# Query projections of head pairs by seven products, and values made per group, in a decoder layer on one core

## The chip, the cores and the metric

The kernel runs on one core of one Trainium2 chip. The metric is the device time of one execution in microseconds. Before the change three runs gave 1305.65, 1307.67 and 1308.76 us; their median, 1307.67, is the time before. The core's engines are called as the profile calls them: PE (TensorE matmul), PEld (its weight load), DVE (VectorE), ACT (ScalarE), POOL (GpSimd) and SP (SyncE, which issues most DMAs).

## What is computed

The reference is one decoder layer on 1024 positions of width 512, all in float32: attention with 32 query heads and 8 key and value heads of width 128, rotary positions and a causal mask; a layer norm; a gated feed-forward part of inner width 1792; a second layer norm.

```
q = (x @ wq)  -> 32 heads;   k = (x @ wk), v = (x @ wv) -> 8 heads
q = q * cos + rotate_half(q) * sin;   k likewise
att = softmax(mask(q k^T / sqrt(128)));   out = (att v) @ wo
x = layernorm(x + out)
n = rmsnorm(x) * ln_w
x = layernorm(x + down(silu(gate n) * up n))
```

Each key and value head serves four query heads, which are called a group here; there are eight groups, 0 to 7.

## The kernel before

Positions are cut into eight tiles of 128 (`T`, `NT`) and each tile into four blocks of 32 rows (`Q`). One step of the attention, a slot, takes 32 positions of all four heads of a group as one 128-row product: `scores(g, t, ...)` multiplies `qT[:, t]` (four heads x 32 positions) with the keys up to that position, DVE adds the mask and takes the row minimum (`low`), ACT takes the exponential, DVE the reciprocal of its sum, ACT scales, DVE transposes in 32x32 blocks (`turned`). After four slots a tile is whole; 16 DMAs on SP bring it into position order (`gather`, `moved`), and PE multiplies it with the values (`o`). Two tiles then go together through the output projection, as seven products for a two by two block product (`project_pair`), added into `sums` by DVE. Tiles are taken in the order 7, 1, 5, 3, 4, 2, 6, 0 in every group.

PE's instructions stand in the order in which the program emits them. The other engines' order is set by a scheduler, close to the program's order. A small planner decides what PE does between the scores of one slot and the next. It counts in units of about one 512-wide matmul call. Work is of two kinds. `Late` pieces are the value product and output projection of a tile whose gather should have landed. `Early` pieces are the projections for the next group, as a fixed list from `projections(g + 1)` and the values. Each slot has a budget, its share by weight of all units of the group; the weight of block t is 1 - share + 2 share (t + 1) / 33, with share 0.25 for groups 0 to 5. In `run`, late work that is due comes first, then early work up to a pace (`early.total * passed / slots`, `passed` being the weights so far). Early work behind `must` (the total less 2.5 units for each slot still to come) is emitted at the slot's end whether there is room or not, so after a group's last slot all of it is out. Groups 6 and 7 use `deal`, which spreads what is left.

`project` makes one projection of 512 positions of one head: four calls over the four 128-row chunks of x (`xT`), then on DVE the product with the cosines (L335) and, halves swapped, with the sines (L337, L338), all read from PSUM, then on POOL the sum of both (L339). A group's list is: both halves of the keys, the queries of four heads for positions 512 to 1023, then for 0 to 511. Queries of a group fill one of two buffers `qTs` (pool `qp`). `values` (L298) makes the values of two groups at once: x's 128 positions are the weights, and 256 columns of `wv` move. It is called in portions of four or eight tiles.

Before the first group, `xT` and the first weights are loaded on the queues of SP and ACT, and PE projects the keys and queries of group 0 in full: 40 calls. PSUM has four single banks for projections, outputs and values (`mbank`) and two double banks for scores (`pair`): scores of one slot reuse the bank of the slot two before, when ACT has taken its exponential. The queue of SP also carries the weights, issued when the tile that they go to is to be free. The feed-forward part follows after the eight groups and runs PE with products of 512 columns to the end.

## Time and profile before

| what | value |
|---|---|
| runs | 1305.65, 1307.67, 1308.76 us (median 1307.67) |
| profiled execution | 1307.23 us, span 1305.4 us |
| PE busy | 1288.0 us, 99% of the span |
| DVE, ACT, POOL busy | 754.3, 463.0, 346.6 us |
| mean granted PE clock | 0.995 |
| start up to the first scores | 40.45 us |
| a group in the middle (2 to 5) | 125 to 126 us |
| longest waits of PE (s for ACT p) | 8.9 us in 6 waits, all in groups 6 and 7 |

Busy PE is a pipelined measure: a 512-wide instruction is recorded as 0.59 us long but follows the one before by 0.43 us. So the time of a stream of matmuls is read from starts. A call in the program is two instructions in these rows, as the operands are float32. Idle time of DVE, ACT and POOL costs nothing by itself; what counts is whether PE, whose order is fixed, finds its operands and its bank ready.

### The profile page before, as it was taken

Reading aid. Unit: us, or ns where it says so; the run is one execution under the profiler, and the core shown is the slowest. Engines: PE = TensorE matmul, PEld = TensorE weight load, DVE = VectorE, ACT = ScalarE, POOL = GpSimd, SP = SyncE. Lnnn points to the kernel's source line nnn. Section 1 sums busy time; section 2 is a strip of 40 time slices with the busy share of each in tenths; the row PEclk is TensorE's granted clock in tenths of the full one; section 3 lists DMA queues with packets and bytes.
Section 4 is the critical chain, followed back from the end, with each engine's and each line's share of the span. In section 5 each row is a group of like instructions: output and inputs, shape, how many; then the busy total and the mean of one; then the engine's idle time right before and its main releaser. Section 6 shows DMA issues by size and latency. Waiting matters only on the chain. (4 is left out here: it accounts for less than half of the span.)

```text
span 1305.4 us, 13447 instructions
## 1 busy us (share of the span) xinstructions
PE 1288.0 (99%) x3842; PEld 717.6 (55%) x3842; DVE 754.3 (58%) x1570; ACT 463.0 (35%) x927; POOL 346.6 (27%) x557
## 2 busy tenths in 40 slices
PE   9999999999999999999999999999999999999998
PEld 4655655655565556555655565554656544444445
DVE  4666566566656775577567656666656564244122
ACT  0443344434443444344444443445454021121000
POOL 6222214112312331242123212331411444423000
PEclk9999999999999999999999999999999999999999
DMA  8242324334333433343234323444344511100000
GB/s 281 69 113 69 89 77 125 81 98 114 96 85 90 113 92 82 89 126 93 73 88 114 91 71 81 122 105 108 92 106 112 179 37 49 44 17 1 16 25 24
DMA packets 102120, 115.48 MB, mean 88 GB/s; under 512 B 18976, under 2 KB 77088, under 8 KB 102048
## 3 DMA queue, kind: packets, MB, share of 16 engines
q1 hardware_dynamic: 101040, 112.67, 32.8%
q10 hardware_dynamic: 1008, 1.97, 0.4%
q8 instruction: 31, 0.51, 0.2%
q14 instruction: 41, 0.34, 0.1%
HBM read 37.23 MB, written 2.10 MB: 30 GB/s over the span
## 5 line engine op out<-in xcount | busy, mean ns | idle before, releaser
L401 ACT ACTIVATE p<-s,low 128x928 f32<-128x928 f32 (+31 forms) x256 | 179.2, 700 | 457.0 <-DVE low L387 425.1
L132 PE MATMUL s<-kT,qT 128*128 128x512 f32 (+15 forms) x768 | 271.8, 464 | 8.9 <-ACT p L401 8.9
L132 PE MATMUL o<-moved,v 128*128 128x512 f32 x550 | 258.5, 599 | 0.0
L409 DVE STREAM_TRANSPOSE turned<-p 128x1024 f32<-128x1024 f32 (+7 forms) x244 | 186.7, 775 | 100.8 <-ACT p L406 84.5
L132 PE MATMUL q_ps<-xT,wq 128*128 128x512 f32 x512 | 240.2, 594 | 0.0
L132 PEld LDWEIGHTS s<-kT,qT 128*128 128x128 f32 x768 | 145.4, 190 | 159.6 <-issue 131.5
L387 DVE CUSTOM_DVE_ANT_0 s<-s,mask 128x928 f32<-128x928 f32 (+31 forms) x256 | 179.7, 704 | 64.0 <-PE s L132 62.2
L406 ACT ACTIVATE p<-p,share 128x928 f32<-128x928 f32 (+31 forms) x256 | 186.0, 734 | 56.5 <-DVE share L405 56.4
L132 PEld LDWEIGHTS o<-moved,v 128*128 128x128 f32 x550 | 103.2, 191 | 103.9 <-issue 97.9
L339 POOL TENSOR_TENSOR qT<-qT,q_b 128x512 f32<-128x512 f32 x64 | 81.0, 1267 | 239.4 <-DVE q_b L338 237.4
L132 PEld LDWEIGHTS q_ps<-xT,wq 128*128 128x128 f32 x512 | 95.6, 191 | 86.8 <-issue 80.8
L405 DVE RECIPROCAL share<-total 128x1 f32<-128x1 f32 x256 | 40.9, 160 | 146.2 <-ACT p L401 145.1
L132 PE MATMUL y<-wo,oT 128*128 128x256 f32 x428 | 104.5, 380 | 0.0
L399 POOL MEMSET p<- 128x96 f32 (+2 forms) x192 | 26.9, 152 | 271.0 <-DVE turned L409 232.3
L132 PE MATMUL f<-wd,hT 128*128 128x512 f32 (+1 forms) x252 | 96.4, 545 | 0.0
L132 PEld LDWEIGHTS y<-wo,oT 128*128 128x128 f32 x428 | 80.0, 190 | 19.9 <-issue 7.3
L132 PEld LDWEIGHTS f<-wd,hT 128*128 128x128 f32 x252 | 47.9, 190 | 48.8 <-issue 47.1
L555 DVE TENSOR_TENSOR sums<-y,sums 128x512 f32<-128x512 f32 x112 | 68.4, 613 | 9.3 <-PE y L132 6.4
L132 PE MATMUL v_ps<-wv,xT 128*128 128x256 f32 x256 | 62.1, 379 | 0.0
L335 DVE TENSOR_TENSOR qT<-q_ps,cos 128x512 f32<-128x512 f32 x64 | 44.0, 687 | 30.0 <-PE q_ps L132 19.2
L132 PE MATMUL k_ps<-xT,wk 128*128 128x512 f32 x128 | 60.2, 593 | 0.0
L132 PEld LDWEIGHTS v_ps<-wv,xT 128*128 128x128 f32 x256 | 48.6, 190 | 16.1 <-issue 8.5
(143 smaller groups left out, 1198.8 us busy)
## 6 DMA issues: line engine op xcount, KB each, us to landing
moved<-turned SPq DMA_DIRECT2D x112, 128.0 KB, 2.4
moved<-turned SPq DMA_DIRECT2D x128, 112.0 KB, 2.2
moved<-turned SPq DMA_DIRECT2D x112, 96.0 KB, 2.1
moved<-turned SPq DMA_DIRECT2D x112, 80.0 KB, 2.1
wq<-wq SPq DMA_DIRECT2D x32, 256.0 KB, 2.8
wo<-wo SPq DMA_DIRECT2D x32, 256.0 KB, 2.9
moved<-turned SPq DMA_DIRECT2D x128, 64.0 KB, 2.0
moved<-turned SPq DMA_DIRECT2D x128, 48.0 KB, 1.9
```

What stands on the lines that cost most here:

```text
L132: tc.keep_in_program_order(nc.tensor.matmul(*args, **kw))
L335: nc.vector.tensor_tensor(dst, like(ps), like(cos[:, ts]), ALU.mult)
L339: nc.gpsimd.tensor_tensor(dst, dst, like(b), ALU.add)
L387: nc.vector.tensor_tensor_reduce(out=s[:, :n], in0=s[:, :n], in1=mask[:, T - n :], scale=1.0, scalar=MASKED, op0=ALU.add, op1=ALU.min, acc ...
L399: nc.gpsimd.memset(p[:, n:full], 0.0)
L401: nc.scalar.activation(p[:, :n], s[:, :n], AF.Exp, bias=low, scale=-1.0, accum_out=total)
L405: nc.vector.reciprocal(share, total)
L406: last_of_all = nc.scalar.activation(p[:, :n], p[:, :n], AF.Copy, scale=share)
L409: nc.vector.transpose(x[:, :, :, b, :].rearrange("p b j q -> p j b q"), p[:, :full].rearrange("p (j b k) -> p j b k", b=B, k=Q),)
L555: pin(nc.vector.tensor_tensor(to, out, to, ALU.add))
```

## The change

For two heads and all positions a query projection is a two by two block product: positions in two halves, x's 512 features in two halves, two heads. The change computes it with seven products and sums (Strassen's scheme in Winograd's form) where eight products stood: `project_two` issues seven products of two calls each. Fifteen of the sixteen head pairs go this way; the last two heads of group 7 stay with `project`.

The two halves of the positions are now the odd and the even tiles (x, cosines and sines are reordered so). The blocks a11, a12 (odd) and a22 (even) and the sums s1 to s4 of x are formed by DVE once at the start and kept; a21 itself isn't kept. Where the plain product of the even tiles is wanted, `operands` gives s1 and a22, and the weight's second half is replaced by its difference to the first, on POOL (`difference`). The sums of the weights of a pair (u1 to u4) are formed on POOL by `weigh`, for the next pair, after product p4. The order of products is p1, p2, p6, p5, p7, p4, p3. From them come c11 (odd, first head), c22 (even, second), c21 (even, first) and c12 (odd, second), in that order. Each is added up by DVE, in place of a read of PSUM by the rotation, and then rotated where it stands (`rotate`); c12 comes after p3, the last.

Queries are kept in three buffers of half a group each, taken in turn by `queries`: the even tiles' queries of the next group take the place of the odd ones of this group. So the planner holds early work back (`odd`) until the four odd tiles have had their scores. Values are made for one group at a time, in two pieces (odd and even tiles) with 128 columns moving, and copied by ACT once a piece. A group's early list is: keys odd, values odd, keys even, values even, then two head pairs; 44 units, where it was 48. Before the first group PE makes keys and queries of group 0 in 36 calls.

Loads of `wq`, `wk` and `wv` are issued at the end of the last use of what they replace. In the last group one spare tile in the place of x holds what had been in two tiles. Tiles in the feed-forward part change places; its products stay.

```diff
-OWN = [0] * (KV - 1) + [2]
+OWN = 2
+BY = 3
...
-    qp = pool("qp", 2)
+    qp = pool("qp", 1)
...
-    cp = pool("cp", 11)
+    cp = pool("cp", 9)
...
-        xT = wide.tile([P, NC, T], F32, tag="wide", name="xT")
+        blocks = wide.tile([P, 7, NC // 2, W], F32, tag="wide", name="blocks")
+        a11, a12, a22, s1, s2, s3, s4 = (blocks[:, n] for n in range(7))
+        a21 = s3
...
+        def weigh(n):
+            if 2 * n >= HEADS - OWN:
+                return
+            a, b = wqs[2 * n], wqs[2 * n + 1]
+            b11, b21, b12, b22 = a[:, :2], a[:, 2:], b[:, :2], b[:, 2:]
+            t = ap.tile([P, 3, NC // 2, HD], F32, tag="uq", bufs=1, name=f"uq{n}")
+            u1, u2, u4, u3 = t[:, 0], t[:, 1], t[:, 2], b12
+            nc.gpsimd.tensor_tensor(u1, b12, b11, ALU.subtract)
+            nc.gpsimd.tensor_tensor(u3, b22, b12, ALU.subtract)
+            nc.gpsimd.tensor_tensor(u2, b22, u1, ALU.subtract)
+            nc.gpsimd.tensor_tensor(u4, b21, u2, ALU.subtract)
+            sums_of[n] = b11, b21, b22, u1, u2, u3, u4
+
+        def difference(w):
+            nc.gpsimd.tensor_tensor(w[:, 2:], w[:, 2:], w[:, :2], ALU.subtract)
+
+        def operands(w, even):
+            x1, x2 = (s1, a22) if even else (a11, a12)
+            return [(w[:, c], (x1 if c < 2 else x2)[:, c % 2]) for c in range(NC)]
...
+        def load_block(queue_of, block, half, c):
+            queue_of.dma_start(
+                block[:, c % 2], x_t[c * P : (c + 1) * P, half * W : (half + 1) * W]
+            )
 
         load_wq(0)
-        load_xT(nc.scalar, 1, 0)
-        load_xT(nc.sync, 1, 1)
-        load_xT(nc.scalar, 1, 2)
+        load_block(nc.scalar, a11, 0, 0)
+        load_block(nc.sync, a11, 0, 1)
+        load_block(nc.scalar, a12, 0, 2)
         load_wk(0)
-        load_xT(nc.scalar, 1, 3)
+        load_block(nc.scalar, a12, 0, 3)
+        for c in range(NC):
+            load_block((nc.scalar, nc.sync)[c % 2], a21 if c < 2 else a22, 1, c)
+        load_wq(1)
         nc.sync.dma_start(sin, rope_sin)
         nc.scalar.dma_start(cos, rope_cos)
-        for c in range(NC):
-            load_xT(nc.scalar if c % 2 == 0 else nc.sync, 0, c)
-        for n in range(1, REP):
-            load_wq(n)
+        load_wq(2)
+        load_wq(3)
         load_wv(0)
-        load_wk(1)
         load_wo(0)
...
+        kTs, vs = {}, {}
+        held_q = qp.tile([P, 3, T // 2 // Q, REP, Q], F32, tag="q", name="queries")
+        def queries(g, even):
+            return held_q[:, (2 * g + even) % 3]
+        nc.vector.tensor_tensor(s1, a21, a22, ALU.add)
+        nc.vector.tensor_tensor(s3, a11, a21, ALU.subtract)
+        nc.vector.tensor_tensor(s2, s1, a11, ALU.subtract)
+        nc.vector.tensor_tensor(s4, a12, s2, ALU.subtract)
+        weigh(0)
+        def values(g, even):
+            if g not in vs:
+                vs[g] = piece(f"v{g}").rearrange("p (j f) -> p j f", j=NT)
+            if even:
+                difference(wvs[g])
+            pv = mbank(f"v_ps{g}_{even}")
+            for j in range(NT // 2):
+                for c, (w, x) in enumerate(operands(wvs[g], even)):
+                    matmul(
+                        pv[:, j * HD : (j + 1) * HD],
+                        lhsT=x[:, j * P : (j + 1) * P],
+                        rhs=w,
+                        start=(c == 0),
+                        stop=(c == NC - 1),
+                    )
+                if j == NT // 2 - 1:
+                    nc.scalar.copy(
+                        vs[g][:, 1 - even :: 2, :], pv.rearrange("p (j f) -> p j f", f=HD)
+                    )
+                    if even:
+                        load_wv(g + 1)
+                yield NC * HD / W
...
+        def rotate(dst, src, even, name):
+            ts = slice(even * W, (even + 1) * W)
+            b = ap.tile([P, W], F32, tag="rope_b", name=f"{name}_b{even}")
+            def swapped():
+                for to, of in ((slice(0, 64), slice(64, P)), (slice(64, P), slice(0, 64))):
+                    nc.vector.tensor_tensor(
+                        alike(b, dst)[to], src[of], alike(sin[:, ts], dst)[of], ALU.mult
+                    )
+            if src is dst:
+                swapped()
+            nc.vector.tensor_tensor(dst, src, alike(cos[:, ts], dst), ALU.mult)
+            if src is not dst:
+                swapped()
+            nc.gpsimd.tensor_tensor(dst, dst, alike(b, dst), ALU.add)
...
+        def project(dst, w, even, name):
+
+            if even:
+                difference(w)
+            ps = mbank(f"{name}_ps{even}")
+            for c, (w_c, x_c) in enumerate(operands(w, even)):
+                matmul(ps, lhsT=w_c, rhs=x_c, start=(c == 0), stop=(c == NC - 1))
                 if c < NC - 1:
                     yield 1
-            b = ap.tile([P, W], F32, tag="rope_b", name=f"{name}_b{h}")
-            shape = "p (n q) -> p n q"
...
+            dst = kTs[g].rearrange("p (n q) -> p n q", q=P)[:, 1 - even :: 2, :]
+            yield from project(dst, wks[g], even, f"k{g}")
+            if even:
+                load_wk(g + 1)
+        def project_queries(g, head, even):
+            dst = queries(g, even)[:, :, head, :]
+            yield from project(dst, wqs[g * REP + head], even, f"q{g}_{head}")
+        def project_two(g, n):
+            b11, b21, b22, u1, u2, u3, u4 = sums_of[g * 2 + n]
+            u = f"{g}_{n}"
+            v = ap.tile([P, W], F32, tag="v", bufs=1, name=f"qv{u}")
+            c11, c12, c21, c22 = (
+                queries(g, even)[:, :, 2 * n + h, :] for even in range(2) for h in range(2)
+            )
+            v_q = alike(v, c11)
+            ps = {}
+            products = (
+                (1, b11, a11), (2, b21, a12), (6, u2, s2), (5, u1, s1), (7, u3, s3),
+                (4, u4, a22), (3, b22, s4),
+            )
+            for k, w, x in products:
+                ps[k] = mbank(f"q{u}_p{k}")
+                q = alike(ps[k], c11)
+                for c in range(NC // 2):
+                    matmul(
+                        ps[k], lhsT=w[:, c], rhs=x[:, c], start=c == 0, stop=c == NC // 2 - 1
+                    )
+                    if c < NC // 2 - 1:
+                        yield 1
+                if k == 1:
+                    nc.scalar.copy(v, ps[1])
+                elif k == 2:
+                    nc.vector.tensor_tensor(c11, q, v_q, ALU.add)
+                    rotate(c11, c11, 0, f"q{u}_0")
+                elif k == 6:
+                    nc.vector.tensor_tensor(v, ps[6], v, ALU.add)
+                elif k == 5:
+                    nc.vector.tensor_tensor(c12, q, v_q, ALU.add)
+                elif k == 7:
+                    nc.vector.tensor_tensor(v, ps[7], v, ALU.add)
+                    nc.vector.tensor_tensor(c22, alike(ps[5], c22), v_q, ALU.add)
+                    rotate(c22, c22, 1, f"q{u}_1")
+                elif k == 4:
+                    nc.vector.tensor_tensor(c21, q, v_q, ALU.add)
+                    rotate(c21, c21, 1, f"q{u}_0")
+                    weigh(g * 2 + n + 1)
+                else:
+                    nc.vector.tensor_tensor(c12, q, c12, ALU.add)
+                    rotate(c12, c12, 0, f"q{u}_1")
+                    for h in range(2):
+                        load_wq((g + 1) * REP + 2 * n + h)
+                yield 1
...
+            pieces = [(NC, f(g, even)) for even in range(2) for f in (project_keys, values)]
+            pieces[1::2] = [(NT // 2 * NC * HD / W, p) for _, p in pieces[1::2]]
+            for n in range(REP // 2):
+                if 2 * (g * 2 + n) < HEADS - OWN:
+                    pieces.append((PAIR * 2, project_two(g, n)))
+                else:
+                    pieces += [(NC, project_queries(g, 2 * n + h, 0)) for h in range(2)]
+            return pieces
...
                 k1 = min(n, k0 + W)
                 matmul(
                     s[:, k0:k1],
-                    lhsT=qT[:, t, :, :].rearrange("p h q -> p (h q)"),
+                    lhsT=queries(g, i % 2 == 0)[:, i // 2 * B + b].rearrange("p h q -> p (h q)"),
...
+                if first and keep and k == 2:
+                    both[g, k] = [rows(f"held{k}_{n}") for n in range(2)]
                 elif first:
+                    if keep:
+                        t = piece(f"held{k}")
+                    else:
+                        t = ap.tile([P, 2 * W], F32, tag="oT", name=f"oT{u}")
+                    both[g, k] = [t[:, :W], t[:, W:]]
+                oT = both[g, k][p % 2]
...
+        def deal(early, limit, coming, weights, must, cap):
...
+                elif early.done < min(cap, early.there()):
...
-        keys, queries = projections(0)[:2], projections(0)[2:]
-        for _, piece_of in queries[:1] + keys[::-1] + queries[1:]:
-            for _ in piece_of:
+        pieces = [piece_of for _, piece_of in projections(0)]
+        for _ in range(4):
+            next(pieces[4])
+        for k in (0, 2, 4, 5):
+            for _ in pieces[k]:
                 pass
         for g in range(KV):
-            todo = [(NC, project_queries(g, a, 0)) for a in range(REP - OWN[g], REP)]
-            own = NC * OWN[g]
+            todo, own, odd = [], 0, math.inf
             if g == 0:
-                todo += some_values(0, range(NT))
+                todo += [(NT // 2 * NC * HD / W, values(0, even)) for even in range(2)]
...
             if g + 1 < KV:
+                odd = sum(units for units, _ in todo) + 2 * (NC + NT // 2 * NC * HD / W) + 9
                 todo += projections(g + 1)
-            m = g // 2 + 1
-            if m < KV // 2:
-                half = some_values(m, range(4) if g % 2 == 0 else range(4, NT))
-                todo[-3:-3] = half
+            else:
+                todo += [(NC, project_queries(g, a, 1)) for a in range(REP - OWN, REP)]
+                own = NC * OWN
             early = Early(todo, held if g == KV - 1 else ())
...
-                if p == 1 and g % 2 == 0 and g // 2 + 1 < KV // 2:
-                    load_wv(g // 2 + 1)
-                if p == 4 and g + 2 < KV:
-                    load_wk(g + 2)
...
-                        run(due, early, pace, must, LEAST)
+                        if g == 0:
+                            must = max(must, min(NC * 2, done))
+                        run(due, early, pace, must, LEAST, odd if done < slots // 2 else None)
-                        deal(early, limit, coming, weights[done - 1 :], own * min(1, done / 3))
+                        must = own * min(1, done / BY)
+                        cap = min(limit, odd) if done < slots // 2 else limit
+                        deal(early, limit, coming, weights[done - 1 :], must, cap)
...
-        nT = wide.tile([P, NC, T], F32, tag="wide", name="nT")
+        normed = wide.tile([P, 7, T], F32, tag="wide", name="normed")
+        nT = normed[:, :NC]
...
+
+    order = np.arange(T).reshape(NT // 2, 2, P)[:, ::-1].transpose(1, 0, 2).ravel()
+        "x_t": given["L0_attn_x"].reshape(T, HID)[order].T,
+        "rope_cos": cos[:, order],
+        "rope_sin": sin[:, order],
```

## The prediction, made before the changed kernel had run

> **What bounds the kernel now.** I read the page first: busy time by engine, then the costliest groups. TensorE (PE) is busy for 1288.0 of 1305.4 us. In the group rows, DVE and POOL sit beside it with idle time of their own.
>
> ```profile
> PE 1288.0 (99%) x3842; PEld 717.6 (55%) x3842; DVE 754.3 (58%) x1570; ACT 463.0 (35%) x927; POOL 346.6 (27%) x557
> L132 PE MATMUL q_ps<-xT,wq 128*128 128x512 f32 x512 | 240.2, 594 | 0.0
> L339 POOL TENSOR_TENSOR qT<-qT,q_b 128x512 f32<-128x512 f32 x64 | 81.0, 1267 | 239.4 <-DVE q_b L338 237.4
> L132 PE MATMUL v_ps<-wv,xT 128*128 128x256 f32 x256 | 62.1, 379 | 0.0
> L335 DVE TENSOR_TENSOR qT<-q_ps,cos 128x512 f32<-128x512 f32 x64 | 44.0, 687 | 30.0 <-PE q_ps L132 19.2
> ```
>
> Second, the busy time by stretch. For two whole head groups PE has no gap, and DVE works 81 of 125 us. Work taken from PE there is time gained, and every wait put before PE is time lost.
>
> ```profile
> 287.80:414.20 126.40, 126.36 (x397) 73.50 (x397) 81.12 (x174) 53.61 (x108) 32.32 (x55) 1.00 0.39 99
> 539.60:665.00 125.40, 125.40 (x394) 72.90 (x393) 81.16 (x174) 53.62 (x108) 32.39 (x55) 1.00 0.39 99
> ```
>
> Third, the timeline of PE, DVE and POOL where group 1 hands over to group 2. The last projection (two calls, four instructions) starts at 290.42. The next group's first scores follow at 292.14, without a wait, while DVE and POOL still rotate that projection until 295.77. That is free because these rows are for positions 0 to 511, and the first tile is tile 7. In rows of one engine the columns are start, duration, engine, line, operation and operands.
>
> ```profile
> 287.61 0.38 PE L132 MATMUL s<-kT,qT 128*128 128x128 f32 x2
> 287.83 1.03 PE L132 MATMUL y<-u,os 128*128 128x256 f32 x4
> 290.42 1.88 PE L132 MATMUL q_ps<-xT,wq 128*128 128x512 f32 x4
> 292.14 1.72 PE L132 MATMUL s<-kT,qT 128*128 128x512 f32 x4
> ...
> 292.34 0.69 DVE L335 TENSOR_TENSOR qT<-q_ps,cos 128x512 f32<-128x512 f32 x1 [1.29 <-PE q_ps L132]
> 293.05 0.69 DVE L337 TENSOR_TENSOR q_b<-q_ps,sin 64x512 f32<-64x512 f32 x1
> 293.75 0.68 DVE L338 TENSOR_TENSOR q_b<-q_ps,sin 64x512 f32<-64x512 f32 x1
> ...
> 294.52 1.25 POOL L339 TENSOR_TENSOR qT<-qT,q_b 128x512 f32<-128x512 f32 x1 [6.34 <-DVE q_b L338]
> ```
>
> Fourth, the same view of the start. PE projects from 5.61 to 40.45 and starts scores at once. DVE waits for the cosines until 11.74.
>
> ```profile
> 40.45 1.72 PE L132 MATMUL s<-kT,qT 128*128 128x512 f32 x4
> 42.01 2.32 PE L132 MATMUL v_ps<-wv,xT 128*128 128x256 f32 x10
> 44.16 1.77 PE L132 MATMUL s<-kT,qT 128*128 128x512 f32 x4
> ...
> 11.74 0.69 DVE L335 TENSOR_TENSOR qT<-q_ps,cos 128x512 f32<-128x512 f32 x1 [10.61 <-DMA cos<-rope_cos]
> 27.23 0.69 DVE L337 TENSOR_TENSOR q_b<-q_ps,sin 64x512 f32<-64x512 f32 x1 [3.06 <-POOL kT L339]
> ```
>
> Last, what a PE stop does to its clock: stretches of 3.4 us around two stops late in the run (after the total: PE, PEld, DVE, ACT and POOL busy, then clock).
>
> ```profile
> 893.40:896.80 3.40, 1.33 (x6) 0.96 (x7) 1.83 (x11) 2.48 (x6) 0.00 (x0) 1.00 0.45 152
> 896.80:900.20 3.40, 3.40 (x6) 1.42 (x5) 2.06 (x6) 1.43 (x7) 0.46 (x3) 0.52 0.30 70
> 992.40:995.80 3.40, 2.39 (x8) 1.14 (x6) 2.25 (x6) 1.60 (x2) 0.00 (x0) 1.00 0.35 106
> 995.80:999.20 3.40, 2.24 (x8) 1.43 (x9) 1.83 (x9) 3.19 (x10) 0.00 (x0) 1.00 0.00 0
> ```
>
> A stretch with 1.33 us of work was followed by one at half clock. Stretches with 2.39 and 2.24 were not.
>
> **The change part by part.** The sum is made against the profiled execution, 1307.2 us (span 1305.4 and 1.8 around it); the median of the runs shown is 0.4 above.
>
> *Query products.* From start to start, an instruction 512 wide takes 0.43 us (four from 290.42 to 292.14), and a call is two. A pair of heads falls from 16 calls to 14, so 2 x 2 x 0.43 = 1.72 us less. Two of the 15 pairs are in the start, counted there; 13 x 1.72 = 22.3 us less.
>
> *Values.* 256 instructions 256 wide (ten from 42.01 to 44.16: 0.215) become 512 instructions 128 wide (two from 287.61 to 287.83: 0.11): 55.0 becomes 56.3, +1.3 us. Bounds +0.9 and +1.7, at 0.109 and 0.111. The Trainium skill, "TensorE: Matmul & The Clock Gate", Back-to-back issue gap, gives some 81 ns for each matmul of a sustained stream 128 wide; by that page values would cost 41 us, 14 less than before; the row of this float32 kernel says 110 ns, and I take the row.
>
> *The handover.* The planner's order follows from its units. A group now has 44 early units (16 keys and values, 28 products). Before its last slot the pace is 44 x 31.19/32 = 42.9, so 43 are done; the last slot first takes late output products, then is forced to finish. The last PE work before the next group's first scores is thus the second call of p3 (both calls, from group 0 to 1). p3 completes c12: odd tiles, second head. Tile 7 is odd, and its scores read all four heads of one row block. PE must therefore stand until c12 is rotated. From the rows: DVE starts 0.63 us after the last instruction's start (291.71 to 292.34); one new add 0.69; three rotation steps 0.61 to 0.70 each (they now read SBUF; nearest row on DVE with both inputs there is 1.225 for 1024 columns); POOL 0.09 later, 1.25; some 0.06 to PE. That is 4.6 to 4.8, less the 0.43 that PE needed anyway: 4.2 us. Lower bound 3.7 (today's chain, 295.83 - 292.14, no extra add). Upper 6.6, if POOL first forms the next pair's weight sums (4 x 0.73, the 128x256 row). No gain is possible: a read-after-write stands there. Then the clock: a stop of 4.2 us leaves over 2 us idle in some 3.41 us window, and a half-clock window costs at most 1.7, less where it overlaps the stop: 0.6 to 1.7, I take 1.5. Groups 0 to 5 hand over so: 6 x 5.7 = +34.2 us, bounds 6 x 3.7 = 22 (no window caught) and 6 x 8.3 = 50. From group 6 to 7 the last projection ends before tile 0's scores and three output products, where PE already waits 2.3 us: nothing added, at most 4.
>
> *The start.* Before the first scores PE now has 36 calls, not 40. But DVE has four sums of x (1.22 each, the 1024-column row), two key rotations (6 x 0.69), and per pair seven adds and twelve rotation steps (4.8 + 7.3 to 8.3): 33 to 35 us, where it had ten rotations of 2.06. The sums of x wait for the last of x; that is 2.5 MB into the queues, as the cosines were, so about 11.7 (wq, x and wk first, 1.5 MB, then x's other half where sines and cosines stood). DVE ends at 45 to 47 and POOL adds 1.35. POOL itself has 34 us to do (today's 25.7 busy in the first 40, and the weight sums of three pairs, 8.8), and DVE has waited for it up to 3.06 us at a time. First scores at 46 to 53; I take 49 for 40.45: +8.5, and 1 for the clock after a stop of some 12 us.
>
> *Within groups.* DVE gets 14 adds of 0.69, about 8.3 net of cheaper steps, on 81 of 125 us; POOL 7.3 (weight sums and differences) on 32. They hide in DVE's and POOL's idle time; p7's burst (two adds and a rotation, 3.3 us) delays the masking of scores behind it, and PE's next-but-one scores with it. Behind POOL's differences stand the even keys and values. Today scores in groups 1 to 5 come 1.6 to 7 us after their buffer is free, so most of that is covered: +3, bounds 0 and 15. Loads moved to the end of their last use go through SP a group ahead of need, behind the gathers already issued; 2.8 us to landing against about 100, so 0, and 3 each if the slack were gone. Banks turn over every two calls, not four, inside the same 3 us. The last group, its spare buffers and the feed-forward part keep their order: 0. The Trainium skill, "SBUF — State Buffer", Who interferes with whom, speaks against the change: a DVE instruction with two SBUF inputs and a POOL instruction that reads SBUF block each other, and all new rotations have two. By it each of 180 steps could wait up to 1.25 us; no row of before shows such a pair, and it is not in the sum.
>
> Sum: 1307.2 - 22.3 + 1.3 + 34.2 + 9.5 + 3 = 1332.9, so 1333 us.
>
> **The rivals.** *The handover costs nothing* (faster): if other PE work lands between p3 and the scores, the start still loses: 1333 - 34.2 = 1299. For it: late products often lie there within a group. Against: today's order at all of these handovers is projection, then scores. It decides at 8.2/6 = 1.4 us each. *Neither start nor handover loses* (faster): 1307.2 - 25.8 + 1.3 = 1283; against it stands DVE's 33 us of work after 11.7. *DVE becomes the bound inside groups*: with its waits for ACT it is blocked longer than its 81 us. If half of the 8.3 us a group reaches PE, that is 7 x 4.15 = 29 more, less the 3 already counted: 1359. *The 128-wide matmuls run at the weight loads' duration* of 190 ns: 97 us for 55, 1374; against it, the 0.11 above.
>
> **How the numbers follow.** Forecast 0.64 (own range 1316 to 1352, from the bounds), free handover 0.14, all gain kept 0.05, DVE bound 0.15, wide loads 0.02. The range 1298 to 1358 leaves out the 0.05, half of the 0.14 and half of the last two. Faster by over 0.2% (2.6 us, what this kernel's measurement can tell): 0.19; within: 0.02; slower: 0.79.
>
> **What would show it.** Right: at six handovers, PE's scores wait about 4 us on POOL's rotation add, and the clock falls to half for 3.4 us; first scores near 49 us; query products 14 calls a pair; groups some 2 us longer than 125. Wrong: scores within 1.4 us of p3 at handovers, or first scores near 37.

## The result, and the profile after

The changed kernel takes 1386.99 us (median of four runs, 1383.66 to 1388.53) where the kernel before takes 1307.16 in the same comparison. The ratio is 1.0607, with a 95% interval of 1.0583 to 1.0632: 80 us slower, where 26 were forecast. The profiled execution took 1387.9 us, with a span of 1385.7 and a mean granted PE clock of 0.968 (before: 1305.4 and 0.995).

Rows of the page after, busy time and groups:

```profile
PE 1294.5 (93%) x4038; PEld 723.7 (52%) x4038; DVE 848.5 (61%) x1679; ACT 466.2 (34%) x926; POOL 436.4 (31%) x635
...
L132 PE MATMUL s<-kT,queries 128*128 128x512 f32 (+15 forms) x768 | 285.8, 483 | 73.3 <-POOL queries L389 54.6
...
L380 DVE TENSOR_TENSOR q_b<-queries,sin 64x512 f32<-64x512 f32 x120 | 113.9, 949 | 3.4
...
L389 POOL TENSOR_TENSOR queries<-queries,q_b 128x512 f32<-128x512 f32 x64 | 88.0, 1378 | 158.1 <-DVE queries L386 143.6
...
L132 PE MATMUL v_ps<-wv,blocks 128*128 128x128 f32 x512 | 63.8, 278 | 0.0
```

PE's idle time stands before the scores, and POOL's rotation add ends most of it. The values' row went from 62.1 to 63.8 us. A rotation has one step with the cosines and two with the sines. Priced at 0.61 to 0.70 us each, the sine steps take 0.949 in the mean (the cosine step 0.735). The keys' rotation reads PSUM, and its sine steps still take what they took:

```profile
L380 DVE TENSOR_TENSOR k_b<-k_ps,sin 64x512 f32<-64x512 f32 x32 | 22.0, 688 | 0.6
```

Matmul starts give a second account. Where an instruction doesn't wait, it follows the one before by the width's own pitch (0.43 us for 512 columns, 0.11 for 128). The sum of these pitches is the time PE needs; what lies above it is lost. Before, PE needed 1272.9 us and lost 26.3. After, it needs 1248.2 and loses 130.5. So the matmuls became 24.7 us cheaper, and 104 us of stops and slow clock came in. The starts of each group's first scores on PE show where:

| | first scores, groups 0 to 7 (us) |
|---|---|
| before | 40.5, 165.0, 292.1, 417.8, 543.2, 668.6, 794.1, 900.8 |
| after | 61.5, 189.4, 324.7, 460.6, 595.2, 730.5, 865.5, 980.6 |

The start is 21.0 us later, the seven groups up to group 7's first scores together 58.8 us longer, and everything behind that 0.5. The largest single places are the handovers. Here are PE, then DVE, then POOL of the changed kernel where group 2 hands over to group 3 (start, duration, engine, line, operation):

```profile
452.76 1.02 PE L132 MATMUL q_p<-blocks,wq 128*128 128x512 f32 x2
460.60 3.46 PE L132 MATMUL s<-kT,queries 128*128 128x512 f32 x4 [6.82 <-POOL queries L389]
...
446.96 2.04 DVE L380 TENSOR_TENSOR q_b<-queries,sin 64x512 f32<-64x512 f32 x2
...
450.36 2.23 DVE L380 TENSOR_TENSOR q_b<-queries,sin 64x512 f32<-64x512 f32 x2
...
456.34 0.65 DVE L457 TENSOR_TENSOR queries<-q_p,queries 128x512 f32<-128x512 f32 x1
457.10 1.39 DVE L380 TENSOR_TENSOR q_b<-queries,sin 64x512 f32<-64x512 f32 x2
458.52 0.69 DVE L386 TENSOR_TENSOR queries<-queries,cos 128x512 f32<-128x512 f32 x1
...
449.67 1.24 POOL L247 TENSOR_TENSOR wq<-wq 128x256 f32<-128x256 f32 x1
...
453.14 2.92 POOL L389 TENSOR_TENSOR queries<-queries,q_b 128x512 f32<-128x512 f32 x2
...
459.29 1.25 POOL L389 TENSOR_TENSOR queries<-queries,q_b 128x512 f32<-128x512 f32 x1 [2.97 <-DVE queries L386]
```

The last projection instructions are p3's, and the scores stand behind c12, as forecast. From c12's add on DVE (456.34) to the scores it is 4.3 us, where the forecast's steps give 3.9 to 4.2. But that add starts 3.15 us after p3's last instruction (453.19, 0.43 after 452.76), not 0.63; over the six handovers it is 3.1 to 3.8. DVE is late with c22 and c21, and what stands behind them in its order (masks, sums of the output projection) is late with them. Their pairs of sine steps take 2.04 and 2.23 us beside POOL's weight sums (0.73 forecast, 1.24 here). With POOL idle, c12's pair takes 1.39. The stretches of 3.4 us show how full both engines were (total, then PE, PEld, DVE, ACT and POOL busy, then clock):

```profile
446.00:449.40 3.40, 3.40 (x16) 2.45 (x15) 3.32 (x6) 0.00 (x0) 3.40 (x4) 1.00 0.79 185
449.40:452.80 3.40, 3.40 (x19) 3.01 (x18) 3.33 (x7) 0.00 (x0) 3.24 (x4) 1.00 0.78 182
452.80:456.20 3.40, 0.98 (x3) 0.15 (x1) 3.37 (x11) 1.67 (x6) 3.40 (x6) 1.00 0.59 136
456.20:459.60 3.40, 0.00 (x0) 0.00 (x0) 2.86 (x5) 0.00 (x0) 0.43 (x3) 0.50 0.06 16
459.60:463.00 3.40, 2.40 (x3) 1.17 (x4) 0.00 (x0) 0.00 (x0) 0.94 (x1) 0.50 0.11 27
463.00:466.40 3.40, 3.40 (x7) 2.02 (x6) 1.61 (x3) 1.02 (x2) 0.00 (x0) 0.50 0.09 24
```

DVE and POOL have next to no idle time for 10 us; then PE stops, and its clock is at half until 466. Over the six handovers the stops are 43.0 us (6.9 to 7.6 each), and the half clock behind them costs 14.8.

The start, on PE, has two large stops, one for the difference of the key weights on POOL and one for the last rotation:

```profile
21.05 3.78 PE L132 MATMUL k_ps<-blocks,wk 128*128 128x512 f32 x4 [5.90 <-POOL wk L254]
...
61.46 2.77 PE L132 MATMUL s<-kT,queries 128*128 128x512 f32 x3 [12.59 <-POOL queries L389]
```

### The profile page after: what moved, and what is told of

Read it like the earlier page. It is cut to its first block, busy times and chain, and to the rows that moved or that the text cites. A ratio compares the mean times of both kernels' runs of the same rounds, so it can differ in the third digit from the quotient of the medians.

```text
span 1385.7 us, 13978 instructions
## 1 busy us (share of the span) xinstructions
PE 1294.5 (93%) x4038; PEld 723.7 (52%) x4038; DVE 848.5 (61%) x1679; ACT 466.2 (34%) x926; POOL 436.4 (31%) x635
## 5 line engine op out<-in xcount | busy, mean ns | idle before, releaser
L132 PE MATMUL s<-kT,queries 128*128 128x512 f32 (+15 forms) x768 | 285.8, 483 | 73.3 <-POOL queries L389 54.6
L132 PEld LDWEIGHTS s<-kT,queries 128*128 128x128 f32 x768 | 145.6, 195 | 231.6 <-issue 130.8
L132 PE MATMUL o<-moved,v 128*128 128x512 f32 x550 | 258.8, 601 | 0.2 <-issue 0.2
L132 PEld LDWEIGHTS o<-moved,v 128*128 128x128 f32 x550 | 103.2, 192 | 103.3 <-issue 98.0
L389 POOL TENSOR_TENSOR queries<-queries,q_b 128x512 f32<-128x512 f32 x64 | 88.0, 1378 | 158.1 <-DVE queries L386 143.6
L132 PE MATMUL q_p<-blocks,wq 128*128 128x512 f32 x240 | 122.3, 619 | 1.8 <-DVE qv L445 1.7
L380 DVE TENSOR_TENSOR q_b<-queries,sin 64x512 f32<-64x512 f32 x120 | 113.9, 949 | 3.4
L132 PE MATMUL y<-wo,oT 128*128 128x256 f32 x428 | 104.3, 380 | 0.0
L132 PEld LDWEIGHTS y<-wo,oT 128*128 128x128 f32 x428 | 80.3, 190 | 20.6 <-issue 7.2
L132 PE MATMUL q_p<-blocks,uq 128*128 128x512 f32 x180 | 85.1, 600 | 0.6 <-DVE queries L442 0.6
L132 PE MATMUL k_ps<-blocks,wk 128*128 128x512 f32 x128 | 63.1, 619 | 6.3 <-POOL wk L254 5.9
L132 PEld LDWEIGHTS q_p<-blocks,wq 128*128 128x128 f32 x240 | 45.5, 197 | 43.9 <-issue 37.4
L132 PEld LDWEIGHTS v_ps<-wv,blocks 128*128 128x128 f32 x512 | 63.2, 195 | 6.2 <-issue 4.6
L132 PE MATMUL f<-wd,hT 128*128 128x512 f32 (+1 forms) x162 | 64.8, 545 | 0.0
L132 PE MATMUL v_ps<-wv,blocks 128*128 128x128 f32 x512 | 63.8, 278 | 0.0
```

Source lines behind the costliest of these rows:

```text
L132: tc.keep_in_program_order(nc.tensor.matmul(*args, **kw))
L380: nc.vector.tensor_tensor(alike(b, dst)[to], src[of], alike(sin[:, ts], dst)[of], ALU.mult)
L389: nc.gpsimd.tensor_tensor(dst, dst, alike(b, dst), ALU.add)
```

## The experiments

Three explanations stood against each other at first. Theory A: the order of the products, with c12 last, and a late start make the loss. The rivals put it elsewhere: in the three half buffers, their hold on early work and the faster turn of the banks, or in work on DVE and POOL that no order mends. Each expectation uses the letters A to C for theories of its own. Times against the kernel before are given with an interval where several rounds were run; the others are single runs beside runs of before of 1305 to 1309 us.

### Product p3 before p7 and p4 (e1_odd_first)

```diff
-                (1, b11, a11), (2, b21, a12), (6, u2, s2), (5, u1, s1), (7, u3, s3),
-                (4, u4, a22), (3, b22, s4),
+                (1, b11, a11), (2, b21, a12), (6, u2, s2), (5, u1, s1), (3, b22, s4),
+                (7, u3, s3), (4, u4, a22),
...
-                odd = sum(units for units, _ in todo) + 2 * (NC + NT // 2 * NC * HD / W) + 9
+                odd = sum(units for units, _ in todo) + 2 * (NC + NT // 2 * NC * HD / W) + 11
```

Now the even tiles' queries come last, and tile 7 doesn't need them. The loads of the next weights move to p4 with the end of the pair, and the planner's hold (`odd`) moves up by p3's two calls, which no longer have to wait for it.

> Product p3, which completes the odd tiles' queries, is taken before p7 and p4 instead of last; the work is the same. Theory A (the handover waits because c12 is last, behind DVE's backlog): six waits of 7.0 us and the half-clock windows after them, some 2.4 each, go: 56 us less, and first scores up to 8 us earlier than 61; some 1323 us, 1318 to 1340 if DVE's work put off at the start comes back. Theory B (the wait is for the three half buffers, whose places are reused): the order doesn't matter, 1387, within 5. Theory C (DVE is simply overloaded in each group): the waits move to other scores and the time stays above 1365.

It took 1327.24 us: 60 of the 80 us are gone. PE's waits for POOL's rotation add fell from 54.6 us in seven to one, at the start:

```profile
PE s L132 <- ACT p L510: 14.2, 12, 3.3
PE k_ps L132 <- POOL wk L254: 6.4, 1, 6.4
PE y L132 <- DVE qv L449: 4.5, 5, 0.9
PE s L132 <- POOL queries L389: 3.8, 1, 3.8
```

First scores stand at 52.1, 174.4, 299.6, 425.5: the groups are back at 122 to 127 us, with the buffers untouched. Order is shown to be the largest single cause.

### No weight sums on POOL (e2_no_weight_sums)

```diff
-            t = ap.tile([P, 3, NC // 2, HD], F32, tag="uq", bufs=1, name=f"uq{n}")
-            u1, u2, u4, u3 = t[:, 0], t[:, 1], t[:, 2], b12
-            nc.gpsimd.tensor_tensor(u1, b12, b11, ALU.subtract)
...
+            sums_of[n] = b11, b21, b22, b12, b22, b12, b21
```

> POOL forms no sums of weights (60 instructions left out); the products take the raw weight blocks, so the queries are not the layer's. All else as in the changed kernel. Theory A (DVE's rotation steps with two SBUF inputs are slowed by POOL's reads: 0.95 us in the mean where rows from PSUM took 0.69): steps fall to 0.75 to 0.85, handover waits from 7.0 to some 5, first scores from 61 to some 54; 1365 us. Theory C (DVE's load alone): steps and waits unchanged, 1380 to 1387.

It took 1372.57, 14 less than the change. The handover stops did not shrink as this run's theory A had said (42.8 us against 43.0), so the weight sums do not set their length. The first scores came at 57.6 instead of 61.5, and a sine step took 0.895 instead of 0.949. Without the sums the step still was not back at 0.69: POOL's other adds and differences were left, and at the handover c21's pair took 2.36 us beside the add of c22's rotation, which now runs there in place of the weight sums.

### Group 0 made plainly (e4_plain_start), and with the new order (e5_both)

```diff
+            if g == 0:
+                heads = [(a, even) for even in range(2) for a in range(REP)]
+                return [project_keys(0, even) for even in range(2)] + [
+                    project_queries(0, a, even) for a, even in heads
+                ]
```

> Only group 0's queries are made as before the change, four calls each, the odd tiles' first; groups 1 to 7 as in the changed kernel. If the start's 21 us are DVE's and POOL's work on two head pairs before the first scores, first scores come at 41 to 44 and the time is 1366 to 1370. If the start waits for x's blocks and sums, they stay later than 50 and the time above 1375. Handover waits stay at 7.0 in either case.

1370.38 us; the total was met, the start was not: first scores at 48.3, not 41 to 44. PE waited 5.3 us for the key weights' difference on POOL. That stood behind a sum of `wo`, which waited for the DMA of `wo`, which nothing at the start needs:

```profile
12.12 1.49 POOL L254 TENSOR_TENSOR wq<-wq 128x256 f32<-128x256 f32 x1
17.35 1.26 POOL L281 TENSOR_TENSOR u<-wo,wo 128x512 f32<-128x512 f32 x1 [3.75 <-DMA wo<-wo]
18.57 1.26 POOL L388 TENSOR_TENSOR queries<-queries,q_b 128x512 f32<-128x512 f32 x1
19.78 0.74 POOL L254 TENSOR_TENSOR wk<-wk 128x256 f32<-128x256 f32 x1
```

The next kernel has both edits, order and plain start:

> p3 before p7 and p4, and a plain start. If the two costs add: 1387 - 56 - 20 = 1311, 1300 to 1320, about the time before the change; the products' 22 us would then be spent on what is left within groups. If they don't add (DVE's load comes out elsewhere): above 1330.

1322.27 us (four runs), ratio 1.0117 [1.0100, 1.0133]. That is above the 1300 to 1320 expected if the two costs add, and something was left within the groups. PE lost 60.5 us where before lost 26.3.

### The loads of wo and of later x behind the start (e7_wo_later on the change, e6_both_wo_later on e5_both)

```diff
-        load_wo(0)
-        for k in range(NT // 2):
-            load_x(k)
...
+        load_wo(0)
+        for k in range(NT // 2):
+            load_x(k)
         for g in range(KV):
```

> The changed kernel, with one move: loading of the first output weights, their sums on POOL and the residual's loads come after group 0's projections. In the changed kernel the difference of the key weights stands on POOL behind the first of these sums, which waits for its load, and PE waits 5.9 us for it in the start, with 2 more at half clock. If that is so: no such wait, first scores from 61 to 53 or 54, and 1379 to 1381 us. If the start is bound by DVE's work alone: first scores within 2 us of 61, and 1385 to 1387.

1390.26 on the change itself: no gain, with first scores at 64.3, later than before the edit (61.5). A miss, and the reading behind it was wrong. The stop for the key weights stayed, 5.4 us where the change has 5.9:

```profile
PE s L132 <- POOL queries L386: 55.0, 7, 13.6
...
PE k_ps L132 <- POOL wk L254: 5.4, 1, 5.4
```

With seven-product pairs in the start, the first pair's weight sums stand on POOL before the difference, with or without the sums of `wo`; in the change itself POOL waited only 0.49 us for the DMA of `wo`.

> Plain start, p3 before p7 and p4, and the first output weights after the start. First scores from 48.1 to 40.5 or 41, as before the change, and 1322 - 7.5 = 1314.5 us, 1312 to 1318. What then stays above 1307 less the saved 21 lies within groups: waits for banks and scores behind DVE, 3 us a group.

1316.50 us (four runs), ratio 1.0061 [1.0044, 1.0078], first scores at 40.6. On a plain start the same edit is worth 5.8 us. This is the mended kernel that the later runs start from. It still carries twelve seven-product pairs in groups 1 to 6 and one in group 7, and is 9 us above the kernel before.

### Two SBUF operands beside POOL (m1_ports, and e9_rotate_psum on the change)

The Trainium skill, "SBUF — State Buffer", Who interferes with whom, says that a DVE instruction with two SBUF inputs contends with a POOL instruction that reads SBUF, and calls this an exclusive lock. The first kernel is nothing but such streams, 16 instructions of each, one engine alone or both together.

```diff
+    for n in range(16):
+        keep(nc.gpsimd.tensor_tensor(g, e, f, ALU.subtract))
+    for n in range(16):
+        keep(nc.vector.tensor_tensor(d[64:], a[:64], b[:64], ALU.mult))
...
+    for n in range(16):
+        keep(nc.gpsimd.tensor_tensor(g, e, f, ALU.subtract))
+    for n in range(16):
+        keep(nc.vector.tensor_tensor(d[64:], ps[:64], b[:64], ALU.mult))
```

> Not the layer: sixteen instructions of a kind on DVE and on POOL, alone and side by side, in seven stretches. If the two engines share SBUF reads (theory A): DVE's 64x512 product with both inputs in SBUF takes 0.69 us alone and 1.0 to 1.4 beside POOL's 128x256 difference (0.73 alone, 1.0 to 1.4 beside); DVE's product from PSUM and SBUF stays at 0.69 beside POOL, and so do the product from SBUF beside POOL's memset, and the transpose (one input). If they don't: all stay within 0.05 of their time alone.

```profile
L129 DVE TENSOR_TENSOR d<-a,b 64x512 f32<-64x512 f32 x16 | 17.1, 1069 | 0.5
L127 POOL TENSOR_TENSOR g<-e,f 128x256 f32<-128x256 f32 x16 | 16.7, 1041 | 1.2
...
L132 POOL TENSOR_TENSOR g<-e,f 128x256 f32<-128x256 f32 x16 | 11.6, 723 | 1.2
L124 POOL TENSOR_TENSOR g<-e,f 128x256 f32<-128x256 f32 x16 | 11.6, 722 | 1.2
...
L121 DVE TENSOR_TENSOR d<-a,b 64x512 f32<-64x512 f32 x16 | 11.0, 685 | 0.6
...
L134 DVE TENSOR_TENSOR d<-ps,b 64x512 f32<-64x512 f32 x16 | 10.9, 684 | 0.6
```

Alone, DVE's step takes 685 ns (L121) and POOL's 722 (L124). Together they take 1069 and 1041 (L129, L127). With one operand in PSUM, DVE takes 684 beside POOL and POOL 723 (L134, L132): nothing is lost. So the page is right here about who meets whom. A lock held for the whole of each instruction isn't what these streams show: one after the other they are 11.0 and 11.6 us of work, 22.6 together, and side by side they took 17.1 and 16.7. The measurement decides: each took about half of its own length more. The other edit lets the change's rotations read the product's bank and not the sum in SBUF, for all four results (one is shown). The sums are still formed, the queries are not the layer's, and a rotation takes its cosine step first.

```diff
...
-                    rotate(c12, c12, 0, f"q{u}_1")
+                    rotate(c12, q, 0, f"q{u}_1")
```

> The rotations of the two-head products read a product's bank in PSUM in place of the sum in SBUF (so the queries aren't the layer's); each sum is still formed, and the number of instructions is the same. Theory A (steps slowed by two SBUF inputs beside POOL): steps from 0.95 to 0.69, DVE's backlog before c12 shorter, handover waits from 7.0 to 4.5 or 5, clock loss the same; first scores some 8 us earlier; 1387 - 6 x 2.3 - 8 - a few = 1360. Theory C (number of instructions): steps may fall, but waits stay within 0.5 us, and 1380 or more.

```profile
L389 POOL TENSOR_TENSOR queries<-queries,q_b 128x512 f32<-128x512 f32 x64 | 80.9, 1263 | 170.8 <-DVE q_b L380 170.4
...
L380 DVE TENSOR_TENSOR q_b<-q_p,sin 64x512 f32<-64x512 f32 x120 | 82.6, 688 | 1.8
```

1349.92 us, 37 below the change, lower than expected. Sine steps and POOL's adds are back at 0.688 and 1.263. The six handovers cost 26.9 us of stop (4.4 to 4.9 each) and 10.4 of clock. That is 37.3 together, where the forecast had 34.2 and the change has 57.8. The step that the forecast had wrong is back where it was forecast: in five of the six handovers c12's add starts 0.63 us after p3's last instruction. Here is the handover from group 2 to 3 (PE, then DVE; the last instruction starts 0.43 after 433.53):

```profile
433.53 1.02 PE L132 MATMUL q_p<-blocks,wq 128*128 128x512 f32 x2
438.79 2.05 PE L132 MATMUL s<-kT,queries 128*128 128x512 f32 x2 [4.24 <-POOL queries L389]
...
434.59 0.69 DVE L457 TENSOR_TENSOR queries<-q_p,queries 128x512 f32<-128x512 f32 x1
```

First scores came at 54.0 instead of 61.5. So contention made 20.5 us of the handovers and 7.4 of the start. Of the 38.0 us between the two profiled executions, some 10 more came from within the groups.

### What is left: products out, or rotations from PSUM (e12_no_two, e11_both_psum)

Both start from e6_both_wo_later. The first has no seven-product pair at all; odd and even tiles, three buffers, kept sums of x and values by group stay.

```diff
-            for n in range(REP // 2):
-                if 2 * (g * 2 + n) < HEADS - OWN:
-                    pieces.append((PAIR * 2, project_two(g, n)))
-                else:
-                    pieces += [(NC, project_queries(g, 2 * n + h, 0)) for h in range(2)]
+            last = REP - OWN if g == KV - 1 else REP
+            pieces += [(NC, project_queries(g, a, 0)) for a in range(REP)]
+            pieces += [(NC, project_queries(g, a, 1)) for a in range(last)]
```

> Plain start, first output weights after it, and in groups 1 to 7 too every head by four calls a half, the odd tiles' first: no seven products, no sums of query weights, no adds on DVE. What is left of the change is the odd and even tiles, the differences, the three buffers and values per group. PE has 22.3 us more to do than in the version with products and a mended order and start (1316.5). If the products still gain after the mending: 1316.5 + 22.3 = 1339, at least above 1325. If DVE's adds and its contention with POOL eat them: 1308 to 1318, the same or faster.

1307.03 us (ten runs), ratio 0.9991 [0.9981, 1.0000]. The rest of the change costs nothing once order, start and loads are mended. By the matmuls' pitches the seven-product pairs take 22.4 us out of PE's work (1274.0 to 1251.6), and yet they make this kernel 9.5 us slower: 32 us are eaten. The second kernel makes the rotations of the mended kernel read PSUM, as in e9.

> The mended version (1316.5) with rotations that read a product's bank, not the sum (so the queries aren't the layer's): no DVE step with two SBUF inputs. If what is left within groups is contention with POOL: steps 0.69, and 1316.5 - 12 = 1304, 1300 to 1308. If it is the number of DVE's instructions or PSUM banks: 1313 to 1317.

1306.84 us: contention is about 10 of the 32. Some 22 remain.

### The last add on DVE instead of POOL (e10_add_dve)

```diff
-            nc.gpsimd.tensor_tensor(dst, dst, alike(b, dst), ALU.add)
+            add = nc.vector if src is dst else nc.gpsimd
+            add.tensor_tensor(dst, dst, alike(b, dst), ALU.add)
```

> The mended version (1316.5) with the last add of the two-head rotations on DVE instead of POOL: 52 instructions of 1.27 us leave POOL, 52 of 0.7 us come to DVE, and the steps of one rotation meet no add of the rotation before. If contention matters more than DVE's load: 1308 to 1313. If load matters more: 1318 to 1326.

1330.92 us (four runs), ratio 1.0183 [1.0168, 1.0198]. DVE's busy time rose from 819.0 to 848.9 us and the time by 14.4. POOL had 65 us less. In this trade DVE's load costs more than the relief of POOL gives, and more than was expected (1318 to 1326).

### No sums on DVE, and p5's bank emptied early (e14_no_adds, e15_p5_psum, e16_p5_out)

```diff
-                    nc.vector.tensor_tensor(c11, q, v_q, ALU.add)
-                    rotate(c11, c11, 0, f"q{u}_0")
+                    rotate(c11, q, 0, f"q{u}_0")
...
-                    nc.vector.tensor_tensor(v, ps[7], v, ALU.add)
-                    nc.vector.tensor_tensor(c22, alike(ps[5], c22), v_q, ALU.add)
-                    rotate(c22, c22, 1, f"q{u}_1")
+                    rotate(c22, q, 1, f"q{u}_1")
```

> The mended kernel with all pairs, but the rotations read the products in PSUM and DVE makes none of the sums between products (this leaves out part of the computation: the queries are single products, not the sums; ScalarE copies out the products that nothing else reads). DVE loses some 8 us a group, and reads fewer banks. With sums on DVE and rotations from PSUM it was 1306.8 against 1285 by PE's own work plus the loss of 24.5 of the plain kernel, 22 us too many. If DVE's load makes those 22 us, this run comes to 1285 to 1292. If they come from the banks that the products hold or the pace at which the fillers are dealt out, it stays at 1300 to 1308.

1288.03 us: 18.8 of the 22 come back, and most of the products' gain shows (19.0 us against e12_no_two, where the pitches give 22.4). This run also freed p5's bank early, which the sums hold until p7 has come. To tell the two apart, the next two keep the sums and let ACT copy p5 out at once, the first on e11_both_psum, the second on e6_both_wo_later:

```diff
+                    r = ap.tile([P, W], F32, tag="rope_b", name=f"qr{u}")
+                    nc.scalar.copy(r, ps[5])
...
-                    nc.vector.tensor_tensor(c22, alike(ps[5], c22), v_q, ALU.add)
+                    nc.vector.tensor_tensor(c22, alike(r, c22), v_q, ALU.add)
```

> All pairs by seven products, mended, rotations from PSUM with the sums still formed (so the queries are not the layer's: the rotations read single products), and now ScalarE copies product p5 out of its bank at once; before, p5's bank was held over p3 and p7 until DVE had added p7. The same kernel without the copy took 1306.8 with 20.7 us of stops before output and value products (o and y), which wait for a bank; without DVE's sums and with early copies 1288.0 with 3.3. If p5's bank is what they wait for, this gives 1290 to 1297. If DVE's load empties banks late whichever it is, it stays at 1302 to 1309.

> The mended kernel with all pairs (1316.5) and ScalarE's copy of p5, nothing left out; the add into c22 now reads two SBUF operands. If p5's bank was it: 1300 to 1306. If DVE's load: 1314 to 1320.

1306.69 and 1316.89 us, against 1306.84 and 1316.50 without the copy: nothing. So the cost comes with DVE's sums, and not with p5's bank. Whether it is DVE's time for them, or the other products' banks that they hold, was not taken apart; e14_no_adds changes both. One group in the middle, from first scores to first scores, in e6_both_wo_later and then in e14_no_adds (total, then PE, PEld, DVE, ACT and POOL busy):

```profile
413.40:539.20 125.80, 123.20 (x417) 72.09 (x416) 90.09 (x190) 54.11 (x108) 42.09 (x65) 1.00 0.38 97
```

```profile
402.70:524.90 122.20, 122.20 (x417) 72.45 (x416) 80.10 (x175) 56.26 (x112) 39.26 (x65) 1.00 0.39 100
```

With DVE at 90 of 126 us, PE stops for 2.6 us of the group. At 80 of 122 it doesn't stop. The mended kernel's waits over the whole execution say where: scores (s) for the exponential, which waits for DVE's masking; output products (y) for a bank that DVE empties; value products (o) for the gather's DMAs, which start when DVE has transposed. In e14_no_adds most of this is gone (last line):

```profile
PE s L132 <- ACT p L511: 16.3, 14, 3.3
PE y L132 <- DVE qv L445: 4.5, 5, 0.9
PE o L132 <- DMA moved<-turned: 4.3, 4, 1.9
...
PE s L132 <- ACT p L502: 7.3, 6, 2.6
```

In e16_p5_out the output products' waits for DVE are gone, and the scores' waits have grown from 16.3 to 20.9 us.

### Half of the pairs (e13_half)

In groups 1 to 6 only the second pair of heads goes by seven products, in the mended kernel. Its weight sums are formed at the group's keys, and the planner's hold moves with the new order.

```diff
-            for n in range(REP // 2):
-                if 2 * (g * 2 + n) < HEADS - OWN:
-                    pieces.append((PAIR * 2, project_two(g, n)))
-                else:
-                    pieces += [(NC, project_queries(g, 2 * n + h, 0)) for h in range(2)]
+            pieces += [(NC, project_queries(g, a, 0)) for a in range(2)]
+            if g < KV - 1:
+                pieces.append((PAIR * 2, project_two(g, 1)))
+            else:
+                pieces += [(NC, project_queries(g, a, 0)) for a in range(2, REP)]
+            pieces += [(NC, project_queries(g, a, 1)) for a in range(2)]
```

> The mended kernel (odd pieces first, plain start, wo and later x behind the start: 1316.5 us) with only the second pair of heads of groups 1 to 6 by seven products; the first pair is made plainly. Six seven-product pairs instead of twelve. By the pitches of the matmuls PE has 10.3 us less to do than in the same kernel with none (1307.03). With twelve pairs 22.4 us less to do came out as 9.5 us more. If the cost goes with the number of pairs (each eats 2.7 us and saves 1.9 us), this gives 1307 + 6 x 0.8 = 1312 (1309 to 1315). If the cost comes from DVE and the banks being too full only where a group holds both pairs, six pairs pass nearly free: 1297 to 1303, faster than the kernel before.

1298.84 us (five runs, 1294.94 to 1303.07), ratio 0.9939 [0.9915, 0.9962]: 0.6% faster than the kernel before. Two middle groups:

```profile
411.10:535.40 124.30, 124.19 (x421) 73.12 (x420) 85.23 (x181) 53.70 (x107) 39.47 (x63) 1.00 0.38 98
535.40:659.80 124.40, 124.13 (x421) 73.12 (x420) 85.37 (x181) 53.70 (x107) 39.52 (x63) 1.00 0.38 98
```

PE's pitches fall by 10.3 us against e12_no_two, and 8.2 of that reach the time. The cost doesn't go with the number of pairs: at 85 us of DVE in a group little of the gain is lost, at 90 the whole of it and more. That DVE's load makes this step is argued from these two arrangements; another six pairs were not run.

## Why the prediction was wrong

The direction and the places were right, the sizes were not: 1387 us, where the range ended at 1358. Term by term, on the profiled executions (together +25.7 forecast and +80.7 measured):

| term | forecast | measured |
|---|---|---|
| query products outside the start, and values | -21.0 | -21.3 by PE's pitches (-24.7 less the 3.4 of the start's four calls) |
| six handovers | +34.2 (22 to 50) | +57.8: 43.0 stop, 14.8 half clock |
| start | +9.5 (first scores 46 to 53) | +21.0 (61.5) |
| within groups | +3 (0 to 15) | +23.2, the remainder |

*Query products and values* were right: the PE work fell by what was counted, and the row's price of 110 ns for 128 columns held (112 in the median after).

*The handover* was right in its mechanism: p3 last, c12 needed by tile 7, PE standing until POOL's add; e1_odd_first shows it. Its chain from the add on took 4.3 us, where the forecast's steps give 3.9 to 4.2. The step that failed is "DVE starts 0.63 us after the last instruction's start". DVE came 3.1 to 3.8 us after it, because it was behind with c22 and c21, and 7.2 a handover lies above the upper bound of 6.6. With the contention taken away (e9_rotate_psum) it came 0.63 after it in five handovers and 1.1 in one. The clock cost 2.5 each, not 1.5: PE went on at half clock for 3.7 to 5.8 us after the stop, more than one stretch of 3.4.

*The contention* is the common cause. The prediction quoted the rule and then left it out: "no row of before shows such a pair, and it is not in the sum". It belonged in the bounds of every chain with such steps, and the range had no place for it. Taken away (e9_rotate_psum), the handovers cost 37.3, and the time of 1349.9 lies inside the range. With the rule that it quoted and rows of before it could have been bounded by an estimate: a step that waits out one POOL instruction of 0.73 takes 1.4 instead of 0.69, and the four sine steps of the two rotations before c12 then make DVE 4 x 0.73 = 2.9 us late. Measured, it was 2.5 to 3.1 later than forecast.

*The start* had the right chain, DVE's 33 us and POOL's 34, but at uncontended durations, and it missed POOL's queue: the key weights' difference stood behind the first pair's weight sums, and PE stopped 5.9 us for it. First scores came 12.5 us behind the forecast's 49. Contention is 7.4 of these (e9_rotate_psum, 54.0, still behind the upper bound of 53); the other 5 are about the length of that stop, which no run took out alone. "Behind POOL's differences stand the even keys and values" was written for the groups and not carried to the start.

*Within groups* the step that failed is "They hide in DVE's and POOL's idle time". A mean of 90 busy us in 126 leaves idle time on average only. Each sum is also a bank to be emptied and a delay for masking, and the waits of the mended kernel show PE stopping for both. The rival "DVE becomes the bound inside groups" named this; it gave 1359 and was held at 0.15. In the mended kernel, e14_no_adds against e11_both_psum measures DVE's sums, with the banks that they hold, at 18.8 us, e11_both_psum against e6_both_wo_later the contention at 10. In the change itself some 10 of the 23.2 us go with the contention (e9_rotate_psum); the other 13, still four times the forecast's 3, were not measured apart.

The rival "neither start nor handover loses" was worked out at 1283. With both mended, it still was not reached: 1316.5. Only with contention and DVE's sums gone too did the time come near, at 1288.0.

## What to carry to other kernels

Saving matmul work pays only as far as the engines that add up its pieces have room where the pieces arrive: take half of the saving if that half is free, as half of the pairs here gave -8.2 us and all of them +9.5. Put last among the products the one whose result is needed last; that order alone was worth 60 us. When a DVE step's operands move from PSUM to SBUF, look for POOL's work beside it, and bound the step by the sum of both durations; here that was 1.41 us, the streams took 1.07, and alone the step took 0.69.

## What was not expected of the hardware

- A DVE product of two SBUF operands and a POOL subtraction of SBUF operands, each in a stream of 16, took 1069 and 1041 ns, alone 685 and 722. One operand in PSUM removes it wholly (684 and 723). POOL's memset beside DVE costs neither anything (524 and 685), and DVE's 32x32 transpose beside POOL takes 711, with POOL at 724 (the transpose alone was not run).
- A PE stop of 7 us cost 1.9 to 3.0 us more at half clock, one of 4.4 us 1.6 to 1.8. Among the stops of about 7 us the length did not decide: two of 7.6 us cost 1.9 and 2.3, four of 6.9 to 7.0 us 2.0 to 3.0.
- Stops of only about 2 us were also followed by half clock. Three of 1.9 to 2.1 us before scores of the changed kernel left 1.3 to 1.5 us of PE work in a stretch of 3.4 us, and the next 3.4 us ran at half clock. Here is the first of them:

```profile
275.30:278.70 3.40, 1.33 (x5) 0.54 (x4) 3.38 (x8) 1.39 (x4) 1.69 (x2) 1.00 0.55 136
278.70:282.10 3.40, 3.40 (x6) 1.34 (x5) 3.25 (x7) 1.25 (x4) 3.32 (x5) 0.50 0.37 89
```

- With DVE busy for 68% to 69% of a group (e13_half, groups 1 to 5) PE stopped for 0 to 1.6 us a group, at 71% to 72% (e6_both_wo_later) for 2.6 to 4.0. With the sums formed and no contention (e11_both_psum, 70% to 71%) it was 1.7 to 4.0, and at 65% to 66% (e14_no_adds) 0 to 0.7: the loss does not grow evenly with the load.
